# Layer norm of phase two: the bias moved from ScalarE to GpSimd, the two transposes given their own distance, and a new list of task times

## The chip, the cores and the metric

The kernel runs on one core of a Trainium2 chip. The core has five engines with a queue of instructions each, run strictly in order: TensorE (PE, matrix products; its weight loads are listed as PEld), VectorE (DVE), ScalarE (ACT), GpSimd (POOL) and SyncE (SP, which here only issues DMAs). An instruction starts when the one before it on its engine is out of the way and the semaphores it waits for have arrived. The metric is the device time of one execution in microseconds (us); a profile is one further execution, recorded instruction by instruction.

## The reference

A block of four layers on 4096 tokens (2 sequences of 2048) of 512 channels, all in float32, each with a layer norm in front and a residual around it:

```
x = x + attn_a(layernorm(x))     # RWKV recurrence over the tokens
x = x + ffn(layernorm(x))        # 1376 hidden, weights lut[idx]
x = x + attn_b(layernorm(x))     # Mamba: 1024 channels, 16 states, conv of 4
x = x + ffn(layernorm(x))        # the same weights
layernorm(x) = (x - mean) / sqrt(var + 1e-5)
```

The layer norm of one token is one multiplication and one addition per element: `x * rs + nm` with `rs = (var + eps) ** -0.5` and `nm = -mean * rs`. These two numbers per token are what the change is about.

## The kernel before

**Phases.** Phase one (the function's first `with` block) does the RWKV layer in 8 chunks of 512 tokens, and beside it looks up the weights of the ffn. Phase two does the other three layers in 16 chunks of 256 tokens (two tiles of 128 tokens, `NJ` = 2). The change lies in phase two alone.

**Order.** Phase two is written as a list of tasks with times. `line.at(t, fn, ...)` notes a task, and `Line.emit` calls them in order of time; each task issues its instructions to the engines' queues then and there. So the times fix nothing but the order on each engine; on the chip nobody looks at them. One stage `w` of the loop at the end of the phase is 32 units of time (`SLOTS`), and holds work of four chunks: the scan of chunk w, the output projection and second ffn of chunk w-1, the front of the Mamba layer (input projection, convolution, `x_product`) of chunk w+1, and the first ffn of chunk w+2. The dictionary `AT` holds the offsets of the tasks within the stage. Two tasks whose times come out equal are ordered by the order of `line.at` calls, or by the last bit of the sum `32 * w + offset` where rounding makes the two sums differ.

**The scan.** A stage has 32 items (2 halves of 4 channel tiles, by 4 groups of 4 states). Each item goes through: `grow` (POOL, L895 `db = du * B`, L898 adds the carried state), `decay` twice (ACT, L905, two exponentials into one of 3 PSUM buffers `dA`), `run` twice (DVE: the scan L915, the product with C L916, the copy of the last state L918), `fold` (POOL: L925, on half the items L930, L931, the sum over states). For each half, `step_size` makes the step sizes in two parts q = 0, 1: two products (PE L819), ACT L823 to L829 (with exponentials), `log` (ACT L833, a logarithm, tile `lt`), `correct` (DVE L836, L837, reads and writes `lt`), `close` (POOL L842 `dl`, L843 `du`), `carry` (ACT L850, an exponential, tile `h`), `cut` (POOL L857 `h`, L858). The tables of ScalarE for exponential, silu and logarithm differ, so a change between them issues an ACT_TABLE_LOAD.

**The layer norm** `ln(t, ci, box, to)` comes three times per stage: before the front (offset `frontln`; here "front norm"), before the second ffn (`f2ln`; "f2 norm"), before the first ffn (`f1ln`; "f1 norm"). `stats` (L639, L640 on DVE, L641 to L644 on POOL) gives mean and variance `mv`, then `rs` (add, L641; power, L642), then `nrs = -rs` (L644). `scale` issues for each tile j two ACT instructions: L650 makes `nm = mean * nrs` for 128 tokens, and L651 the normalized tile `xn`. `turn` transposes the tile on PE (4 products with the identity, L656, into PSUM tile `tr`) and copies it to SBUF on ACT (L657). The tiles j = 0, 1 are placed at `scale + 0.1 * j` and `turn + 0.1 * j`.

**Other names.** `x_product` (L795 on PE, then ACT copies L798 `bcs` and L800 `dtl`, then a DMA of `bcs` out and a broadcast back, L878) needs all of `u`, the silu of the convolution (ACT L781; the convolution's taps are DVE L775 on the product L755). `half`, `gate` and `close` of the ffn are L700 (PE, gate `pg` and up `gu`), L718 and L721 (ACT silu into `hT`), L727 and L730 (DVE); `residual` is L677 (PE, `po`) and L681 (DVE). The gate of the Mamba layer is L885 (PE) and L891 (ACT `sg`); `total` is L950 (ACT), the end of a scan half L961, L962 (DVE). Weights come through a ring of 18 buffers by DMAs of SP (L612).

Of the kernel before, what the change touches and what calls it, by code (L numbers as in the profile page):

```python
# [8 lines left out]
F32 = mybir.dt.float32  # L9
I32 = mybir.dt.int32  # L10
AF = mybir.ActivationFunctionType
ALU = mybir.AluOpType
# [3 lines left out]
P = 128  # L16
# [44 lines left out]
def block_kernel(ctx: ExitStack, tc: tile.TileContext, a: dict, out: bass.AP):  # L61
    nc = tc.nc
    V, S, G, PE = nc.vector, nc.scalar, nc.gpsimd, nc.tensor
# [33 lines left out]
    with ExitStack() as pa:  # L97
# [4 lines left out]
        small = pa.enter_context(tc.tile_pool(name="a_small", bufs=2))  # L102
# [23 lines left out]
        for k in range(4):  # L126
# [7 lines left out]
                  y=0.475, x=-3.69, stats=-2.901, stat=0.11, each=0.061, copy=0.089, fmul=0.561,  # L134
                  opened=-3.107, mean=-2.389, scale=-2.198, turn=-2.092, out=4.08, outs=0.018,
                  add=0.096, bits=(-4.21, 29.2), marks=(-4.03, 10.79), ahead=0.472, ff=(13.35,
                  31.01), place=-4.5, places=0.069, ffln=11.025, nextln=7.821, flast=1.489,
                  turned=2.527, fgate=0.173, fdown=2.314, times=0.273)
        NBITS = 8
        line = Line()  # L140
# [399 lines left out]
    with ExitStack() as pb:  # L540
# [13 lines left out]
        small = pb.enter_context(tc.tile_pool(name="b_small", bufs=2))  # L554
# [7 lines left out]
        def load_w():  # L562
# [4 lines left out]
        NJ = TB // P  # L567

        AT = dict(total=0.13, y=1.08, decay=1.1, grow=1.5, fold=2.75, gates=(2.59, 0.82, 24.96,
                  26.99), front=(6.05, 6.48, 7.41, 8.16), f2=(8.75, 8.93, 12.67, 14.17, 14.38,
                  16.88), f1=(21.88, 21.98, 24.35, 24.27, 29.8, 25.63), f2d=16.39, f1d=30.14,
                  x=11.42, step0=20.87, step1=9.48, step=2.56, exp=0.62, log=1.16, fix=2.12,
                  du=3.52, carry=3.52, zero=4.38, proj=2.49, frontln=3.04, f2ln=5.92, f1ln=18.95,
                  store=29.71, taps=1.03, conv=0.04, unit=1.86, add=0.6, silu=-0.29, hT=0.36,
                  scale=0.19, turn=0.82, g1ln=-5.01, g1=-0.28, g1s=1.51, late=8.22, step1a=-6.29,
                  ahead=12.53, spread=2.01, gsilu=0.64, bca=-1.73, step0a=22.65, fronta=(-0.27, 2.4,
                  1.42, 4.18), xa=14.67)
        line = Line()  # L580
        xs = {}

# [47 lines left out]
        def ln(t, ci, box, to=None):  # L630


            def stats():
                box["xnT"] = to if to is not None else tp.tile([P, KC, TB], F32, tag="xnT", name="xnT")
                st = small.tile([P, NJ, 6], F32, tag="st", name="st")
                mv = small.tile([P, NJ, 2], F32, tag="mv", name="mv")
                rs = small.tile([P, NJ, 1], F32, tag="rs", name="rs")
                for j in range(NJ):
                    V.bn_stats(st[:, j, :], xs[ci][j])  # L639
                    V.bn_aggr(mv[:, j, :], st[:, j, :])  # L640
                G.tensor_scalar(rs, mv[:, :, 1:2], EPS, None, ALU.add)  # L641
                G.tensor_tensor(rs[:, :, 0], rs[:, :, 0], mhalf[:, :NJ], ALU.pow)  # L642
                nrs = small.tile([P, NJ, 1], F32, tag="nrs", name="nrs")
                G.tensor_scalar(nrs, rs, -1.0, None, ALU.mult)  # L644
                box["mv"], box["rs"], box["nrs"] = mv, rs, nrs

            def scale(j):
                box["xn", j] = wk.tile([P, C], F32, tag="xn", name="xn")
                nm = small.tile([P, 1], F32, tag=f"nm{j}", name="nm")
                S.activation(nm, box["mv"][:, j, 0:1], AF.Copy, scale=box["nrs"][:, j, :])  # L650
                S.activation(box["xn", j], xs[ci][j], AF.Identity, bias=nm, scale=box["rs"][:, j, :])  # L651

            def turn(j):
                tr = mmp.tile([P, KC, P], F32, tag="mm", name="tr")
                for k in range(KC):
                    PE.transpose(tr[:, k, :], box["xn", j][:, k * P : (k + 1) * P], ident)  # L656
                S.copy(box["xnT"][:, :, j * P : (j + 1) * P], tr)  # L657

            line.at(t, stats)
            for j in range(NJ):  # L660
                line.at(t + AT["scale"] + 0.1 * j, scale, j)
                line.at(t + AT["turn"] + 0.1 * j, turn, j)

        def residual(times, ci, lhsT, src):

            po, n = [], len(times)
            w = [stream.piece(t, t + 0.01, src(i)) for i, t in enumerate(times)]

            def first():
                for j in range(NJ):  # L670
                    po.append(mmp.tile([P, C], F32, tag="mm", name="po"))

            def one(i):
                lw = lhsT(i)
                m = lw.shape[0]
                for j in range(NJ):
                    PE.matmul(po[j], lhsT=lw[:, j * P : (j + 1) * P], rhs=w[i]["w"][:m],  # L677
                              start=(i == 0), stop=(i == n - 1))

            def add(j):  # L680
                V.tensor_tensor(xs[ci][j], xs[ci][j], po[j], ALU.add)  # L681

            line.at(times[0], first)
            for i, t in enumerate(times):
                line.at(t + 0.005, one, i)
            for j in range(NJ):
                line.at(times[-1] + 0.3 + AT["add"] + 0.15 * j, add, j)

        def feed_forward(t_ln, times, td, dtd, ci, layer=1):

            box, hT, ps = {}, {}, {}
            if ci == 1 and layer == 0:
                box["xnT"] = ready[1]
            else:
                ln(t_ln, ci, box)
# [36 lines left out]
            for i, ti in zip(range(0, NF, 2), times):  # L732
                d = 0.65 if i + 1 < NF else 0.3
                for j in range(2):
# [3 lines left out]
                    line.at(tj + 0.005, half, i, j, w)  # L738
                line.at(ti + d + AT["silu"], gate, i)
                line.at(ti + 2 * d + AT["hT"], close, i)  # L740
            residual([td + dtd * i for i in range(NF)], ci, lambda i: hT[i], lambda i: wff[i][:, 2 * C :])

        def front(t_ln, times, tx, ci, box):

            box["xnT"] = ready[ci % 2]
            if ci:
                ln(t_ln, ci, box, ready[ci % 2])
# [35 lines left out]
            for cp, tp_ in enumerate(times):  # L783
                w = [stream.piece(tp_, tp_ + 0.01, a["in_proj"][2 * cp + j]) for j in range(2)]
                line.at(tp_ + 0.005, product, cp, w)
                line.at(tp_ + AT["conv"], copy, cp)
                for j in range(2):
# [205 lines left out]
        for w in range(-1, nchunk + 1):  # L993
            t = SLOTS * w
# [13 lines left out]
            if -1 <= w < nchunk - 1:  # L1008
                boxes[w + 1] = {}
                late = AT["late"] if w == 0 else 0.0  # L1010
# [70 lines left out]
```

## Time and profile before

| | |
|---|---|
| median of 3 executions | 3647.52 us (3642.11 to 3651.19) |
| profiled execution | 3645.21 us |
| its span, first to last instruction | 3643.4 us |
| TensorE clock granted, mean | 0.973 of full |
| phase one | about 0 to 700 us of the span |
| phase two | about 700 us to the end; 16 stages |
| length of a stage in the middle | 177.2 us (DMA of `bcs` issued at 1360.08, 1537.28, 1714.34 us) |

"Busy" of an engine is the time in which one of its instructions ran. A line of the timeline gives start, duration, engine, source line, operation, tiles, shapes, count; in square brackets stands the idle time of the engine before it and the instruction that ended it. "x16" counts records, and a float32 product on PE leaves two records. A line of the waits gives the waiting instruction, the one that released it, the total in us, how often, and the longest.

### The profile page before, as it was taken

To read this page: it belongs to the slowest core of one execution; us is meant where nothing else is said; L and a number is where in the kernel's file an instruction comes from. 1 tells how busy PE (TensorE), PEld (TensorE's weight loads), DVE (VectorE), ACT (ScalarE), POOL (GpSimd) and SP (SyncE) were. 2 spreads that over 40 slices of the span, in tenths; PEclk is the share of its full clock that TensorE was granted. 3 is DMA by queue.
4 is the path that set the end of the run, shared out by engine and by line. 5 is a ranking of instruction groups with operands and counts; after the bars stand their busy time and mean duration, and the time that the engine had idled before them with its cause. 6 is when DMAs were issued, how large, how long until landed. Compare 5 with 4: busy or idle time off the path is not lost. (4 is left out here: it accounts for less than half of the span.)

```text
span 3643.4 us, 43340 instructions
## 1 busy us (share of the span) xinstructions
PE 3398.7 (93%) x12592; PEld 2294.4 (63%) x12592; DVE 3231.3 (89%) x4880; ACT 2739.9 (75%) x4862; POOL 2979.1 (82%) x2803
## 2 busy tenths in 40 slices
PE   7998999887999999999999999999999999998698
PEld 3443444466676767677666766676767676766475
DVE  8999999568999999999999999998989898989882
ACT  5556766578787888888787878787878787878661
POOL 2445666378999999999999999999999999999850
PEclk9999999998999999999999999999999999999799
DMA  3111111254565656565656565656565655664442
GB/s 123 55 55 67 58 67 67 82 199 149 179 196 169 217 165 210 169 208 165 216 165 211 168 201 176 202 180 203 180 192 182 190 183 189 188 192 130 141 143 61
DMA packets 267148, 573.02 MB, mean 157 GB/s; under 512 B 29856, under 2 KB 31520, under 8 KB 266912
## 3 DMA queue, kind: packets, MB, share of 16 engines
q1 hardware_dynamic: 266112, 568.68, 49.0%
q8 instruction: 101, 1.65, 0.2%
q10 hardware_dynamic: 800, 1.57, 0.1%
q14 instruction: 135, 1.11, 0.1%
HBM read 543.66 MB, written 26.48 MB: 156 GB/s over the span
## 5 line engine op out<-in xcount | busy, mean ns | idle before, releaser
L915 DVE TENSOR_TENSOR_SCAN h<-h,db 128x512 f32<-128x512 f32 x1024 | 1252.5, 1223 | 124.6 <-ACT h L905 100.2
L895 POOL TENSOR_TENSOR db<-du,bc 128x1024 f32<-128x1024 f32 x512 | 1207.4, 2358 | 37.1 <-PE y L939 34.5
L905 ACT ACTIVATE h<-dl,acol 128x256 f32<-128x256 f32 x2048 | 956.2, 475 | 303.6 <-DVE hst L918 267.4
L916 DVE TENSOR_TENSOR db<-h,bc 128x512 f32<-128x512 f32 x1024 | 708.1, 691 | 35.9
L925 POOL TENSOR_TENSOR db<-db 128x512 f32<-128x512 f32 x480 | 609.9, 1271 | 0.0
L677 PE MATMUL po<-w,hT 128*128 128x512 f32 x1364 | 601.0, 592 | 0.0
L700 PE MATMUL pg<-xnT,w 128*128 128x256 f32 x2400 | 537.0, 381 | 1.1 <-ACT xnT L657 1.0
L700 PE MATMUL gu<-xnT,w 128*128 128x256 f32 x2400 | 537.6, 379 | 0.0
L700 PEld LDWEIGHTS pg<-xnT,w 128*128 128x128 f32 x2400 | 456.7, 191 | 67.5 <-ACT xnT L657 5.5
L700 PEld LDWEIGHTS gu<-xnT,w 128*128 128x128 f32 x2400 | 456.0, 190 | 68.0 <-issue 6.7
L677 PEld LDWEIGHTS po<-w,hT 128*128 128x128 f32 x1364 | 259.4, 190 | 287.9 <-issue 272.0
L931 POOL TENSOR_TENSOR acc<-db 128x256 f32<-128x256 f32 x480 | 349.3, 728 | 37.6
L403 PE MATMUL ps<-xnT,wrvk 128*128 128x512 f32 x768 | 343.5, 599 | 8.6 <-DVE e L428 8.5
L905 ACT ACT_TABLE_LOAD x206 | 264.3, 1283 | 3.7
L885 PE MATMUL ps<-ready,w 128*128 128x256 f32 x1024 | 235.6, 384 | 29.0 <-DVE x L681 14.5
L403 PEld LDWEIGHTS ps<-xnT,wrvk 128*128 128x128 f32 x768 | 146.7, 192 | 181.6 <-issue 162.8
L755 PE MATMUL ps<-ready,w 128*128 128x256 f32 x1024 | 238.2, 393 | 10.1 <-DMA w<-in_in_proj 8.4
L885 PEld LDWEIGHTS ps<-ready,w 128*128 128x128 f32 x1024 | 195.4, 192 | 73.9 <-DVE x L681 24.4
L677 PE MATMUL po<-w,u 128*128 128x512 f32 x512 | 236.8, 611 | 2.1 <-DVE u L962 2.1
L755 PEld LDWEIGHTS ps<-ready,w 128*128 128x128 f32 x1024 | 202.0, 199 | 45.8 <-issue 12.0
L775 DVE SCALAR_TENSOR_TENSOR ps<-xin,cw,ps 128x256 f32<-128x256 f32 x384 | 187.1, 487 | 29.9 <-ACT ps L769 19.5
L930 POOL TENSOR_TENSOR db<-db,acc 128x256 f32<-128x256 f32 x240 | 174.8, 729 | 18.8
(163 smaller groups left out, 4993.5 us busy)
## 6 DMA issues: line engine op xcount, KB each, us to landing
w<-wff SPq DMA_DIRECT2D x1023, 256.0 KB, 2.7
bc<-bcd SPq DMA_DIRECT2D x256, 512.0 KB, 4.4
w<-in_in_proj SPq DMA_DIRECT2D x256, 256.0 KB, 2.8
w<-in_out_proj SPq DMA_DIRECT2D x128, 256.0 KB, 2.8
w<-wff SPq DMA_DIRECT2D x11, 768.0 KB, 4.4
x<-in_x SPq DMA_DIRECT2D x8, 1024.0 KB, 5.4
x<-x1d SPq DMA_DIRECT2D x32, 256.0 KB, 3.5
out_x<-x SPq DMA_DIRECT2D x32, 256.0 KB, 6.7
```

The source lines that it names most:

```text
L403: PE.matmul(ps, lhsT=wrvk[:, k, lo : lo + P], rhs=chunk["xnT"][:, k, :], start=(k == 0), stop=(k == KC - 1))
L677: PE.matmul(po[j], lhsT=lw[:, j * P : (j + 1) * P], rhs=w[i]["w"][:m], start=(i == 0), stop=(i == n - 1))
L700: PE.matmul(to[:m], lhsT=w[:, k, :m], rhs=box["xnT"][:, k, :], start=(k == 0), stop=(k == KC - 1))
L755: PE.matmul(ps[cp][:, j, :], lhsT=wj[:, k, :], rhs=box["xnT"][:, k, :], start=(k == 0), stop=(k == KC - 1))
L775: V.scalar_tensor_tensor(ps[cp][:, j, :], xin[cp][:, j, i : i + TB], cw[:, c, i : i + 1], ps[cp][:, j, :], ALU.mult, ALU.add)
L885: PE.matmul(ps[:, j, :], lhsT=wj[:, k, :], rhs=box["xnT"][:, k, :], start=(k == 0), stop=(k == KC - 1))
L895: G.tensor_tensor(d, box["du", half][:, c4, :].unsqueeze(1).to_broadcast([P, 4, TB]), bs[half, q], ALU.mult)
L905: S.activation(h[:, n, :], box["dl", half][:, c4, :], AF.Exp, scale=acol[:, 4 * half + c4, col : col + 1])
L915: V.tensor_tensor_scan(flat(h), flat(h), flat(d[:, two, :]), 0.0, ALU.mult, ALU.add)
L916: V.tensor_tensor(d[:, two, :], h, cs[half, q][:, two, :], ALU.mult)
L925: G.tensor_tensor(d[:, 0:2, :], d[:, 0:2, :], d[:, 2:4, :], ALU.add)
L931: G.tensor_tensor(to, d[:, 0, :], d[:, 1, :], ALU.add)
```

## The change

`stats` now makes the bias itself, for both tiles at once, on GpSimd: a product of mean and `rs` and a multiplication by -1, in place of `nrs`. `scale` issues one ACT instruction per tile instead of two. The second tile's `turn` stands `turns` = 0.23 units after the first, where it was 0.1. And nearly all offsets of `AT` are new.

```
-        AT = dict(total=0.13, y=1.08, decay=1.1, grow=1.5, fold=2.75, gates=(2.59, 0.82, 24.96,
-                  26.99), front=(6.05, 6.48, 7.41, 8.16), f2=(8.75, 8.93, 12.67, 14.17, 14.38,
-                  16.88), f1=(21.88, 21.98, 24.35, 24.27, 29.8, 25.63), f2d=16.39, f1d=30.14,
-                  x=11.42, step0=20.87, step1=9.48, step=2.56, exp=0.62, log=1.16, fix=2.12,
-                  du=3.52, carry=3.52, zero=4.38, proj=2.49, frontln=3.04, f2ln=5.92, f1ln=18.95,
-                  store=29.71, taps=1.03, conv=0.04, unit=1.86, add=0.6, silu=-0.29, hT=0.36,
-                  scale=0.19, turn=0.82, g1ln=-5.01, g1=-0.28, g1s=1.51, late=8.22, step1a=-6.29,
-                  ahead=12.53, spread=2.01, gsilu=0.64, bca=-1.73, step0a=22.65, fronta=(-0.27, 2.4,
-                  1.42, 4.18), xa=14.67)
+        AT = dict(total=0.94, y=1.66, decay=1.09, grow=1.51, fold=2.58, gates=(2.5, -0.28, 25.02,
+                  27.07), front=(6.07, 6.51, 7.37, 8.21), f2=(8.68, 8.86, 12.67, 14.05, 14.38,
+                  16.88), f1=(21.55, 21.65, 24.43, 24.17, 30.07, 25.72), f2d=16.48, f1d=30.11,
+                  x=10.74, step0=20.72, step1=9.45, step=2.31, exp=0.42, log=1.48, fix=2.49, du=3.4,
+                  carry=3.48, zero=4.25, proj=2.39, frontln=3.23, f2ln=5.96, f1ln=18.6, store=31.98,
+                  taps=1.03, conv=0.18, unit=1.87, add=0.7, silu=-0.29, hT=0.4, scale=0.43,
+                  turn=1.03, g1ln=-0.46, g1=-0.26, g1s=1.39, late=8.05, step1a=-6.84, ahead=14.42,
+                  spread=2.95, gsilu=0.66, bca=1.47, step0a=22.97, fronta=(-0.56, 2.3, 0.72, 2.94),
+                  xa=15.45, turns=0.23)
...
                 G.tensor_scalar(rs, mv[:, :, 1:2], EPS, None, ALU.add)
                 G.tensor_tensor(rs[:, :, 0], rs[:, :, 0], mhalf[:, :NJ], ALU.pow)
-                nrs = small.tile([P, NJ, 1], F32, tag="nrs", name="nrs")
-                G.tensor_scalar(nrs, rs, -1.0, None, ALU.mult)
-                box["mv"], box["rs"], box["nrs"] = mv, rs, nrs
+                nm = small.tile([P, NJ, 1], F32, tag="nm", name="nm")
+                G.tensor_tensor(nm, mv[:, :, 0:1], rs, ALU.mult)
+                G.tensor_scalar(nm, nm, -1.0, None, ALU.mult)
+                box["rs"], box["nm"] = rs, nm
 
             def scale(j):
                 box["xn", j] = wk.tile([P, C], F32, tag="xn", name="xn")
-                nm = small.tile([P, 1], F32, tag=f"nm{j}", name="nm")
-                S.activation(nm, box["mv"][:, j, 0:1], AF.Copy, scale=box["nrs"][:, j, :])
-                S.activation(box["xn", j], xs[ci][j], AF.Identity, bias=nm, scale=box["rs"][:, j, :])
+                S.activation(box["xn", j], xs[ci][j], AF.Identity, bias=box["nm"][:, j, :], scale=box["rs"][:, j, :])
...
-                line.at(t + AT["turn"] + 0.1 * j, turn, j)
+                line.at(t + AT["turn"] + AT["turns"] * j, turn, j)
```

What the new offsets do to the order, as the two programs' instruction lists show it, in a stage of the middle:

- PE: the transposes of the front norm stand four records of `po` later, with four records between the two tiles. Those of the f1 norm have four records between them. Those of the f2 norm stay together. One gate product L885 moves eight `po` products earlier.
- ACT: the f2 norm's two `xn` have one `decay` between them. In the part of the stage that follows, the exponentials L827 and L829 of q = 0 stand ahead of the last `u` (they stood behind it), and the copies `bcs` and `dtl` and one `decay` stand ahead of the logarithm L833 of q = 0 (they stood behind it).
- ACT, stages 8 to 13 only: two silu L718 that followed each other directly now have a `decay` between them, at two places. The silu and the decay have equal times there (14.05 + 0.65 - 0.29 = 15.5 - 1.09 and 21.55 + 0.65 - 0.29 = 23 - 1.09), and rounding decides; in stages 1 to 7 it decides the other way. Stages 14 and 15 have this at the first place. In the whole program the table loads of ACT go from 601 to 629.
- POOL: in each half of the scan, `close` of q = 1 stands one `grow` earlier in the second half, and `close` and `cut` of q = 1 one whole item earlier in the first half of the next chunk. All else has its old order.
- DVE: one `run` changes places with an end of scan half (L961, L962) or with a single `hT`, `lt` at a few places; the norms' L639, L640 keep their place among the runs.
- SP: the store of a finished chunk stands twelve weight loads and no broadcast load later; two loads of gate weights stand four loads earlier.
- Beginning (stage -1, 0) and end (stage 15 and after): the order differs at single places, among them on PE at the end, where the products L939 (`spread`, the sum over states of the last chunk) stand later among the others.

## The prediction

> **What bounds the kernel now.** I read the engines' sums first. They point at PE:
>
> ```profile
> PE 3398.7 (93%) x12592; PEld 2294.4 (63%) x12592; DVE 3231.3 (89%) x4880; ACT 2739.9 (75%) x4862; POOL 2979.1 (82%) x2803
> ```
>
> This is an average over phases. The second view is the busy time in two middle stages, 1539 to 1893 us:
>
> ```profile
> core 0: us, PE busy (x) PEld busy (x) DVE busy (x) ACT busy (x) POOL busy (x), PEclk, DMA share, GB/s
> 1539.00:1893.00 354.00, 342.70 (x1350) 247.41 (x1349) 323.51 (x533) 288.70 (x528) 338.42 (x339) 1.00 0.61 188
> ```
>
> PE 342.7 and POOL 338.4 of 354: close. What tells them apart is who waits. The third view, the waits in stages 2 to 13 (1184 to 3311 us, 2127 us), POOL's and then PE's largest:
>
> ```profile
> POOL rs L641 <- DVE mv L640: 2.5, 7, 0.7
> POOL dl L842 <- DVE lt L837: 2.5, 1, 2.5
> POOL h L857 <- ACT h L850: 1.9, 5, 0.8
> POOL xin L762 <- DVE ps L775: 1.3, 1, 1.3
> ...
> ```
>
> ```profile
> PE tr L656 <- ACT xn L651: 39.2, 45, 1.6
> ...
> ```
>
> POOL waits 8.2 us in all, 0.7 a stage. Its other gaps are its own step from one instruction to the next: 0.08 us where the next one needs the last one's result. PE idles 62.7 us there, 5.2 a stage (39.2 on this line, 13.3 on L681). So POOL sets the stage length of 177.2 us, and PE's waits cost nothing.
>
> The fourth view, POOL's timeline, shows the norm and the two POOL instructions that could start to wait:
>
> ```profile
> 2556.69 0.22 POOL L641 TENSOR_SCALAR rs<-mv 128x2 f32<-128x2 f32 x1
> 2557.00 0.72 POOL L642 TENSOR_TENSOR rs<-rs,mhalf 128x2 f32<-128x2 f32 x1
> 2557.80 0.24 POOL L644 TENSOR_SCALAR nrs<-rs 128x2 f32<-128x2 f32 x1
> ...
> 2593.59 1.28 POOL L842 TENSOR_TENSOR dl<-dl,lt 128x512 f32<-128x512 f32 x1
> ...
> 2614.61 0.26 POOL L857 TENSOR_TENSOR h<-h,hst 128x32 f32<-128x32 f32 x1
> ```
>
> ACT starts the f2 norm's `nm` right at the end of `nrs`, and then runs without a wait for the next 32 us (its timeline):
>
> ```profile
> 2558.07 0.29 ACT L650 ACTIVATE nm<-mv,nrs 128x1 f32<-128x1 f32 x1 [1.95 <-POOL nrs L644]
> ...
> 2585.03 0.60 ACT L781 ACTIVATE u<-ps 128x512 f32<-128x512 f32 x1
> ...
> 2586.94 0.58 ACT L827 ACTIVATE ps<-ps 128x512 f32<-128x512 f32 x1
> ...
> 2588.05 0.98 ACT L905 ACTIVATE h<-dl,acol 128x256 f32<-128x256 f32 x2
> 2589.04 1.28 ACT L833 ACT_TABLE_LOAD   x1
> 2590.34 0.63 ACT L833 ACTIVATE lt<-w 128x512 f32<-128x512 f32 x1
> ...
> 2594.12 0.36 ACT L798 COPY bcs<-ps 32x256 f32<-32x256 f32 x1
> ...
> 2614.04 0.49 ACT L850 ACTIVATE h<-acol,dl 128x16 f32<-128x16 f32 x2
> ```
>
> DVE takes `lt` on (its timeline):
>
> ```profile
> 2592.82 0.69 DVE L837 TENSOR_TENSOR lt<-lt,ps 128x512 f32<-128x512 f32 x1
> ```
>
> It ends at 2593.51 and POOL's `dl` starts at 2593.59, the 0.08 of a direct follower: `close` is within a tenth of a microsecond of making POOL wait. Likewise L850 ends at 2614.53, and `cut` (L857) starts at 2614.61. So ACT's stretch from the f2 norm to `lt`, and on to `carry`, is a second chain without slack.
>
> **The change part by part.** All sums are against the profiled execution, 3645.2 us, which is 2.3 below the median of 3647.5; I don't correct for that.
>
> *1. POOL gets one instruction per norm*, the product mean times `rs`; the multiplication by -1 takes the place of `nrs`. Phase one has that product, on these engines:
>
> ```profile
> L262 POOL TENSOR_TENSOR nm<-rs,mv x11: 196/203/937, 31.9 to 693.1; 128x4 f32<-128x4 f32 x8, 128x2 f32<-128x2 f32 x3
> ```
>
> 0.203 + 0.083 to a dependent follower = 0.286 us. Of 45 norms, 42 lie where POOL is full (all but the first at 825 us and two at the end): **+12.0**. Low end: the 8.2 us of POOL waits absorb their part, +3.8. High end: each takes the 0.937 of the slowest record, 42 x 1.02 = 42.7. I take the median; three of those records have this very shape.
>
> *2. ACT's stretch from the f2 norm to `lt` of q = 0.* Removed: two L650, 0.33 + 0.31 with their steps, -0.64. Moved ahead of the last `u`: L827 and L829, 2586.94 to 2588.05 = +1.11. So `u` ends 28.03 us after the first `xn` starts. Now the wait that is added: `bcs`, `dtl` and one `decay` stand ahead of the logarithm, and `bcs` needs `x_product`, whose last 20 records need this `u`. PE's timeline:
>
> ```profile
> 2585.68 4.70 PE L795 MATMUL ps<-u,wxp 128*128 128x256 f32 x20 [0.50 <-ACT u L781]
> ```
>
> 28.03 + 0.05 + 4.70 = 32.8 us is the earliest `bcs`. ACT is there at 28.03 + 1.29 (table load) + 0.99 (`decay`) = 30.3: it waits 2.5 us, and behind it on ACT's queue are `lt` and all decays. Then 0.27 + 0.26 + 0.99 + 1.30 + 0.63: `lt` ends at 36.25, before at 32.90 (2558.07 to 2590.97). DVE's L837 and the steps add 0.80: `dl` can start 37.08 us after `xn` starts, which is 0.03 after `nm`. POOL, whose order between the two is unchanged, is there 35.55 us after its last norm instruction (2558.04 to 2593.59). It waits 1.53 us per stage. In stages 1 to 6 and 8 to 14 that is 13 x 1.53 = **+19.9** (in stage 7 the same distance has 1.67 of slack). Low end 0, if `u` comes earlier by that much; high end 3.35 x 14 = 47, the whole delay.
>
> *3. Two more table loads in stages 8 to 14*, between two silu and beside a decay: each 1.29 + 0.07 of step, 2.72 a stage, ahead of `carry` of q = 1. From `lt` to the end of L850 ACT took 23.56 (2590.97 to 2614.53). Minus `bcs` and `dtl` (0.52), minus two decays that now stand elsewhere (1.9): 21.1. So L850 would end 36.25 + 21.1 = 57.4 after `xn`, while POOL reaches `cut` at 56.57 - 0.13 + 1.53 = 57.97 with its own wait at `dl`: no wait in stages 1 to 7. With 2.72 more: 60.1, a wait of 2.2 us; 7 stages, **+15.4**. Low end 0 (the loads lie beside waits of ACT, which has 17 us a stage of its own idle time), high end 7 x 2.72 = 19. In exchange the waits of 0.1 to 0.3 at `cut` go: 13 x 0.2 = **-2.6**.
>
> Here the Trainium skill ("ScalarE: Activation LUTs", "What ACT_TABLE_LOAD costs") speaks against the change more than my row does: a switch is the load and a drain of about 1380 ns, 2.66 us together. In this trace the load at 2589.04 is followed by `lt` 1.30 later, with no drain to be seen. By the page the step would be some 18 us larger, as an estimate.
>
> *4. Costed at nothing.* At the front norm ACT waits 5.56 us for `nrs`, DVE then 3.48 for a decay and PE 1.57 and 0.38 for the tiles; two fewer ACT instructions and spread transposes shorten these (2.3 a stage on PE, with the f1 norm's second tile 0.38). POOL covers it: PE gets to the f2 norm earlier and waits there longer, 4 to 5 us, since that `xn` hangs on POOL. If POOL did not cover it, it would be worth -30 in 13 stages. First half of the scan: `dl` and `cut` have 5.4 to 9.5 us between ACT and POOL; `cut` of q = 1 moved one item earlier (4.65) and keeps some 3.7, with the two loads about 1.1. DVE's changed places: a run later by one 0.7 us instruction, under items that POOL folds some 15 us behind. SP's store behind twelve weight loads, and the gate loads earlier: issue of under 1 us, nothing reads the store. Beginning and end: 0, between -10 and +10, the larger part from L939, which waits 30.8 us for the last chunk before and still has to.
>
> **Sum:** 12.0 + 19.9 + 15.4 - 2.6 = +44.7: **3690 us**.
>
> **The rivals.** Changes under 0.3% (10.9 us) can't be told from none here.
>
> *A. PE sets the stage, and it gets faster (the other side).* Then PE's freed waits count, 2.3 x 13 = 30: 3615. For it: PE's 93%, its largest wait is exactly what the change shortens. Against it: POOL's 0.7 us of waits per stage. It decides from where POOL's idle time per stage exceeds the 0.86 us of its three new instructions and ACT's chain stays hidden; the trace has 0.7 and a `dl` without slack. Chance 0.09.
>
> *B. Only POOL's instruction counts.* ACT catches up, because it drops a wait elsewhere in the stretch, and `dl` doesn't wait: 3645.2 + 12.0 = 3657. For it: ACT is 82% busy. Against it: no wait of ACT lies between the f2 norm and `lt`. Chance 0.14.
>
> *C. The waits spread.* The first half's `cut` runs late in stages 8 to 13 too (up to 2.6 x 7 = 18), or the product on POOL takes 0.94 rather than 0.2 (+31): 3705 to 3740. For it: that cover is down to about 1 us. Chance 0.20.
>
> *D. Nothing measurable happens.* 3645, chance 0.04: terms 1 and 2 both swallowed.
>
> **How the numbers follow.** The forecast holds 0.53, with its own range 3675 to 3705 (one of its two waits half as large or half as large again). Faster by over 0.3%: A, 0.09. Within: D and half of B, 0.11. Slower: the forecast, C and the other half of B, 0.80. The range leaves out A, D, the lower third of B and the top of C: 3655 to 3722.
>
> **What the profile after would show.** POOL's L842 waiting for DVE's `lt` by about 1.5 us per stage, and from stage 8 its L857 for ACT's `h` by about 2.2; ACT waiting for PE at `bcs` (L798) by about 2.5; stages of 179.6 us early and some 181.8 from stage 8; 28 more table loads; `nm` on POOL at 0.20; PE's wait for `xn` gone from the front norm and larger at the f2 norm. I am wrong if the stage stays at 177 to 178, if `nm` takes 0.9, or if ACT has no wait at `bcs`. What would break it most easily is term 2: it is a difference of 1.5 us between two chains of 36.

## The result and the profile after

The changed kernel takes 3727.55 us (median; 3726.3 to 3728.07), the kernel before 3648.78: a ratio of 1.0226 (95% interval 1.0214 to 1.0238), or +79 us where +44.7 was forecast. It lies 5.6 us above the range. The profiled execution has a span of 3725.6 us, 82.2 more than before.

The sums of the engines hardly change; TensorE is busy 27 us longer with the same products:

```profile
PE 3426.0 (92%) x12577; PEld 2314.1 (62%) x12592; DVE 3235.4 (87%) x4880; ACT 2751.1 (74%) x4800; POOL 2987.6 (80%) x2848
```

The 12 stages that were read before (1184 to 3311 us there) now lie at 1199 to 3391. POOL's waits in them (waiting line, releaser, total us, times, longest) were 8.2 us in all and are 65.3:

```profile
POOL dl L842 <- DVE lt L837: 43.2, 13, 4.6
POOL h L857 <- ACT h L850: 14.5, 10, 2.7
POOL rs L642 <- DVE mv L641: 7.6, 6, 2.8
```

With 36 norms of one more POOL instruction (+10.1 us) that is 67 us more for 12 stages; their starts show +65. (The first line counts 13 waits, since the one of stage 2, 3.7 us, ends at the edge of the window; the 12 of stages 3 to 14 make 39.4.) The other 17 us lie ahead of stage 2 (its first `grow` starts 12.5 us later than before) and from stage 14 on.

ACT has two waits that were small or absent before (L765 had 6.5 us in 8 waits, L798 none):

```profile
...
ACT xin L765 <- PE ps L755: 33.4, 24, 2.3
ACT bcs L798 <- PE ps L795: 29.9, 12, 2.5
...
```

The second one is the wait that the prediction named. The first one it did not have. Stage 5 shows where it comes from. PE's timeline around the f2 norm, before:

```profile
1678.84 0.66 PE L656 MATMUL tr<-ident,xn 128*128 128x128 f32 x4 [1.55 <-ACT xn L651]
1679.87 0.66 PE L656 MATMUL tr<-ident,xn 128*128 128x128 f32 x4 [0.38 <-ACT xn L651]
1680.36 8.76 PE L755 MATMUL ps<-ready,w 128*128 128x256 f32 x32
```

and after:

```profile
1704.04 1.12 PE L656 MATMUL tr<-ident,xn 128*128 128x128 f32 x4 [4.15 <-ACT xn L651]
1705.66 1.12 PE L656 MATMUL tr<-ident,xn 128*128 128x128 f32 x4 [0.50 <-ACT xn L651]
1706.56 9.05 PE L755 MATMUL ps<-ready,w 128*128 128x256 f32 x32
```

PE waited 4.15 us for `xn`, where it had waited 1.55. After this wait four transposes take 1.12 us instead of 0.66, and 32 records of L755 take 9.05 us. With a full clock they take 7.07, in most stages of the kernel before; in this stage they took 8.76 there, so the clock was low before too, but only behind the transposes. The windows of the same stretch (busy times, then the granted clock, the DMA share and GB/s) say why:

```profile
core 0: us, PE busy (x) PEld busy (x) DVE busy (x) ACT busy (x) POOL busy (x), PEclk, DMA share, GB/s
...
1702.00:1716.00 14.00, 11.46 (x43) 9.61 (x44) 12.07 (x24) 10.67 (x23) 13.36 (x14) 0.76 0.26 75
...
```

The clock was 0.76 of full there: half from 1703.7 to 1710.6 us and full around that (before: half from 1680.8 to 1684.2). ACT's timeline of the same stage:

```profile
1703.18 0.81 ACT L651 ACTIVATE xn<-x,nm,rs 128x512 f32<-128x512 f32 x1 [4.88 <-POOL nm L646]
...
1712.19 0.59 ACT L765 COPY xin<-ps 128x512 f32<-128x512 f32 x1 [1.87 <-PE ps L755]
...
1732.54 0.60 ACT L781 ACTIVATE u<-ps 128x512 f32<-128x512 f32 x1
...
1737.93 0.36 ACT L798 COPY bcs<-ps 32x256 f32<-32x256 f32 x1 [2.49 <-PE ps L795]
...
1740.73 0.63 ACT L833 ACTIVATE lt<-w 128x512 f32<-128x512 f32 x1
...
```

DVE's and POOL's, at the end of the chain:

```profile
1741.40 0.69 DVE L837 TENSOR_TENSOR lt<-lt,ps 128x512 f32<-128x512 f32 x1 [3.30 <-ACT lt L833]
```

```profile
1742.16 1.27 POOL L842 TENSOR_TENSOR dl<-dl,lt 128x512 f32<-128x512 f32 x1 [3.46 <-DVE lt L837]
```

Read along the chain: L765 starts 1.87 us late, the last `u` ends 29.96 us after `xn` starts (28.03 forecast), `bcs` waits 2.49 (2.5), and `dl` makes POOL wait 3.46 (1.53). The excess at `dl` is the wait at L765. In stage 12 the clock over L755 was better (0.93), L765 waited 0.40, and `dl` 1.95. In both stages the difference is 1.55 to 1.6.

DVE's line bears on a reading of the prediction, that ACT's stretch from the f2 norm to `lt` had no slack before. Before, `lt` was written at 2590.97, and DVE took it at 2592.82, 1.85 us later, without a wait, straight behind its own work (1.57 to 1.86 in the stages 2 to 14). So what met POOL's `dl` within a tenth was DVE's queue, and ACT's stretch had some 1.6 to 1.9 us to spare. The forecast of 1.53 does not use that reading; after the change DVE does wait for `lt` (3.30 us), and ACT's stretch is the one that counts.

### The profile page after: what moved, and what is told of

It is laid out like the page before. It is cut to its first block, busy times and chain, and to the rows that moved or that the text cites. A ratio compares the mean times of both kernels' runs of the same rounds, so it can differ in the third digit from the quotient of the medians.

```text
span 3725.6 us, 43195 instructions
## 1 busy us (share of the span) xinstructions
PE 3426.0 (92%) x12577; PEld 2314.1 (62%) x12592; DVE 3235.4 (87%) x4880; ACT 2751.1 (74%) x4800; POOL 2987.6 (80%) x2848
## 3 DMA queue, kind: packets, MB, share of 16 engines
q10 hardware_dynamic: 800, 1.57, 0.1%
## 5 line engine op out<-in xcount | busy, mean ns | idle before, releaser
L755 PE MATMUL ps<-ready,w 128*128 128x256 f32 x1024 | 257.0, 415 | 9.1 <-DMA w<-in_in_proj 8.5
L755 PEld LDWEIGHTS ps<-ready,w 128*128 128x128 f32 x1024 | 216.5, 213 | 50.4 <-issue 12.0
L885 PE MATMUL ps<-ready,w 128*128 128x256 f32 x1024 | 233.5, 382 | 6.6 <-ACT sg L891 5.7
L885 PEld LDWEIGHTS ps<-ready,w 128*128 128x128 f32 x1024 | 195.9, 192 | 47.8 <-issue 13.4
```

Of the source, the lines that this page charges most:

```text
L755: PE.matmul(ps[cp][:, j, :], lhsT=wj[:, k, :], rhs=box["xnT"][:, k, :], start=(k == 0), stop=(k == KC - 1))
L885: PE.matmul(ps[:, j, :], lhsT=wj[:, k, :], rhs=box["xnT"][:, k, :], start=(k == 0), stop=(k == KC - 1))
```

## The experiments

The theory after the result has four costs: the logarithm behind `bcs` (1.5 us per stage), a slow TensorE clock after the f2 norm's wait (about 1.9), the split silu pairs (2.3 per stage from stage 8), and one more POOL instruction (0.28 per norm). The rivals: the clock is a companion, not a cause; the POOL instruction is what costs; PE or ACT bounds the kernel. Ratios are to the kernel before, run on the same chip.

**1. PE kept busy through the wait.**

```
             def turn(j):
...
+                for k in range(fill * (j == 0)):
+                    PE.matmul(tr, lhsT=ident, rhs=wdt[:, :C], start=True, stop=True)
                 for k in range(KC):
```

`fill` is 7 for the second ffn's norm and 0 for the others.

> The changed kernel, with 7 products of a constant weight added on PE ahead of the f2 norm's transposes in each stage; they write the tile that the transposes then overwrite, so no value changes, and they need nothing from ACT. They fill some 3.3 us of the 4.1 us that PE waits there for xn. Theory: in the changed kernel this wait makes the chip grant half the TensorE clock for a while after it, the transposes and the 32 products L755 come 2 us late, ACT waits for them at L765, and this is added to the wait of POOL's dl. Then here: L755 x32 back at 7.1 us (it took 7.6 to 9.6), the transposes at 0.66 (1.12), ACT's wait at L765 gone, POOL's wait at dl 1.55 instead of 3.4 per stage, time some 25 us shorter: about 3702. Rival: the clock is only a companion and the wait at dl comes from the order of ACT's instructions alone; then dl still waits 3.4 and the time is 3727 or longer by the added products.

Measured: 3708.83 us, ratio 1.0172 (1.0156 to 1.0187); the profiled execution took 3702.01. PE's timeline in stage 5:

```profile
1686.78 6.17 PE L654 MATMUL tr<-wdt,ident 128*128 128x512 f32 x14
1692.79 1.04 PE L656 MATMUL tr<-ident,xn 128*128 128x128 f32 x8
1693.66 7.07 PE L755 MATMUL ps<-ready,w 128*128 128x256 f32 x32
```

and POOL's waits over 1199 to 3391 us (the `dl` of stages 3 to 14; 39.4 in the changed kernel):

```profile
POOL dl L842 <- DVE lt L837: 22.2, 12, 4.2
POOL h L857 <- ACT h L850: 17.3, 15, 2.7
...
```

The seven products took 6.2 us, not the 3.3 that I had reckoned, and so filled the wait whole. The clock over L755 is 1.00 from stage 1 on, L755 takes 7.07 us, and `dl` waits 1.5 us in stages 2 to 6 and 10 to 14. The kernel has more work on PE, and it is faster: the clock is a cause, not a companion. The median is 19 us below the changed kernel's, the profiled execution 25, and some 25 were expected; in stages 1, 8 and 9, where the wait to be filled was shorter (1.9 to 3.3 us), the added products made PE late, L765 waits 0.76 to 1.81, and `dl` still waits over 3.

**2. The logarithm ahead of `bcs` again.**

```
-  x=10.74
+  x=11.42
```

> The changed kernel with x = 11.42 instead of 10.74: the copies bcs and dtl on ACT stand behind the logarithm of q = 0 again; nothing else changes on any engine. Theory (the wait of ACT for x_product ahead of the logarithm makes dl late): lt ends 4.0 us earlier, POOL's wait at dl goes from 3.4 to 0 in each stage, even with the slow clock; L857 in stages 8 to 14 waits about 3 instead of 2.3; time about 3688. Rival: the logarithm is late anyway (the product on POOL and the moved L827, L829 hold the chain), dl still waits over 1.5, time over 3710.

Measured: 3682.41 us, ratio 1.0097 (1.008 to 1.0114). POOL's waits in the same window:

```profile
POOL h L857 <- ACT h L850: 21.0, 18, 2.7
POOL rs L642 <- DVE mv L641: 10.3, 12, 1.6
POOL dl L842 <- DVE lt L837: 5.3, 6, 2.1
```

L765 still waits (33.1 us there), the clock over L755 is still 0.73 to 0.86 in all stages from 2 to 14 but one, and yet `dl` hardly waits. In the changed kernel its wait is L765's plus 1.55 us; here, where it waits at all (stage 8 apart), it is L765's minus 1.5 (0.94 and 2.42 in stage 2). So ACT's chain is 3 us shorter, where 4 were expected, and has 1.5 us of slack, which covers most of the slow clock. The two costs are not separate sums: the clock costs only because the chain has no slack, and the order of `bcs` and the logarithm took that slack. Stage 0 also loses its wait at L857 (4.3 us in the changed kernel): the better part of the changed kernel's late beginning was this same wait, since stage 0 starts 1.9 us late there and stage 1 9.4. (The start of stage 0, behind an unchanged phase one, lies between 757 and 769 us in all these profiles, so the 1.9 may be chance.)

**3. The silu pairs together.**

```
-  f2=(8.68, 8.86, 12.67, 14.05, ...), f1=(21.55, ...)
+  f2=(8.68, 8.86, 12.67, 14.06, ...), f1=(21.56, ...)
```

> The changed kernel with the last bits of two offsets moved (14.05 to 14.06, 21.55 to 21.56), so that in stages 8 to 14 the silu pairs stand together again, 31 table loads per stage; order changes on ACT alone. Theory: POOL's waits at L857 in stages 8 to 14 (2.3 each) go, and some of those at the front norm (7 us in all): 3727 - 15 to 20 = about 3709. Rival: the loads lay beside ACT's own waits, and what L857 waits for is the late logarithm: no change, 3725 to 3729.

Measured: 3701.5 us, ratio 1.0154 (1.0139 to 1.017), 26 us less, somewhat more than expected. POOL's waits:

```profile
POOL dl L842 <- DVE lt L837: 39.7, 12, 4.8
POOL h L857 <- ACT h L850: 1.2, 6, 0.4
POOL rs L642 <- DVE mv L641: 1.1, 1, 1.1
```

Both smaller lines of the changed kernel go: 13.3 and 6.5 us of the 26. Behind the window, L857's waits in stages 14 (2.2 us) and 15 (5.7 to 4.3) go or shrink too; `dl`, with the same 12 stages, is as before (39.7 and 39.4). The last line is not the front norm's, as the expectation has it, but the f1 norm's: it lies 115 to 125 us behind a stage's first `grow`, and DVE, which makes `mv`, waits there for the load of `x`. DVE's line of the changed kernel:

```profile
DVE st L640 <- DMA x<-x1d: 4.5, 6, 1.8
```

The prediction didn't have this wait. Here it goes with the split loads (but for stage 8), but they are not its only cause: runs 2 and 5 have it too, run 5 without any split load.

**4. The bias alone on GpSimd, task times of before.** In the kernel before, and with it one ACT instruction per tile:

```
-  G.tensor_scalar(nrs, rs, -1.0, None, ALU.mult)
+  G.tensor_tensor(nm, mv[:, :, 0:1], rs, ALU.mult)
+  G.tensor_scalar(nm, nm, -1.0, None, ALU.mult)
```

> The kernel before with only the bias formed on GpSimd (product and multiplication by -1 in place of nrs, one ACT instruction per tile), all task times as before. Theory: one more POOL instruction of 0.28 us in 42 norms, and ACT's chain 0.6 us shorter: +12, 3657 to 3661. Rival: this alone moves PE's wait to the f2 norm and brings the slow clock, so that dl waits too: over 3670. Other rival, ACT or PE sets the time: 3648 or less.

Measured: 3649.61 us, ratio 1.0011 (1.0002 to 1.0021): +4.8, where +12 was expected. The product takes its time on POOL:

```profile
L644 POOL TENSOR_TENSOR nm<-mv,rs x45: 194/194/196, 824.9 to 3578.1; 128x2 f32<-128x2 f32 x45
```

but from the start of stage 2 to that of stage 14 only 3.0 us are added, not 10. POOL's waits in the 12 stages fall by 3.4, from 8.2 to 4.8, of them 1.8 at `dl` and L857, which hang on ACT and DVE. The rest is no saving that the record can give to the edit: POOL's other instructions took 3.0 us less in this execution (0.15% of their sum, on another chip), and the steps between them 0.5. By the interval the edit costs between 0.7 and 7.7 us. PE waits once at the f2 norm, for 2.15 us (L754 here is L755 elsewhere):

```profile
1678.86 1.37 PE L655 MATMUL tr<-ident,xn 128*128 128x128 f32 x8 [2.14 <-ACT xn L650]
1680.06 8.76 PE L754 MATMUL ps<-ready,w 128*128 128x256 f32 x32
```

The clock over this line is 0.81 to 0.87 in 9 of the stages 2 to 14, with a wait of 0.05 to 0.27 at L765 and none at `dl`; stage 12 with 0.81 and stage 13 with a full clock both last 177.1 us. With the chain in its old order the slow clock costs nothing.

**5. The first three edits together.**

> The changed kernel with the three edits together: products on PE ahead of the f2 norm's transposes, bcs behind the logarithm, silu pairs unsplit. Theory: no wait at dl, none above 0.3 at L857; what stays of the change is the POOL instruction (+12 at most, +4 as measured alone) and about 1.2 us per stage of POOL's wait for the front norm's mv that showed when bcs alone was moved back: 3650 to 3665. Rival (one of the causes was only a companion of another, or something unnamed costs): 3675 or more.

Measured: 3661.78 us, ratio 1.0033 (1.002 to 1.0046). The waits of POOL from 1184 to 3311 us:

```profile
POOL rs L640 <- DVE mv L639: 8.6, 11, 2.3
POOL h L857 <- ACT h L850: 1.6, 2, 0.9
POOL dl L842 <- DVE lt L837: 1.1, 1, 1.1
```

The first line is the f1 norm's again. 15 us of the 79 are left (12 by the ratio); the three edits, which leave the norm and all other times as in the changed kernel, take away the rest. From the start of stage 2 to that of stage 14 it is 9.1 us more than before, and POOL's 36 added instructions take 10.1 there.

**6. The norm of before, with the new task times.** In the changed kernel, and with it two ACT instructions per tile:

```
-  G.tensor_tensor(nm, mv[:, :, 0:1], rs, ALU.mult)
-  G.tensor_scalar(nm, nm, -1.0, None, ALU.mult)
+  G.tensor_scalar(nrs, rs, -1.0, None, ALU.mult)
```

> The changed kernel with the norm of before (nrs on POOL, nm by two ACT instructions), all new task times kept. Theory: POOL gets 0.86 us per stage back, but ACT's chain from the f2 norm is 0.64 longer, and POOL waits for it at dl: the two nearly cancel, 3720 to 3732. Rival (the instruction on POOL costs its time wherever the waits are): 3727 - 12 = 3715 or less.

Measured: 3727.07 us, ratio 1.0216 (1.0199 to 1.0233): as the changed kernel. POOL's instruction is gone, and its wait at `dl` is larger:

```profile
POOL dl L843 <- DVE lt L838: 49.4, 12, 5.3
...
```

49.4 for 39.4 in the same stages 3 to 14: 0.83 us a stage, of which 0.18 is a longer wait at L765 and the rest the two instructions that ACT's chain got back. POOL's 0.86 a stage that became free went into that wait, so the two nearly cancel, as expected; the run cannot price them apart.

Runs 4 and 6 together separate the two halves of the change. The new norm with the old times is 0.1% slower than the kernel before, the old norm with the new times 2.2%, and both together 2.3%. So the loss comes from the list of task times, and hardly from the move of the bias.

**7 and 8. POOL given less work, from the kernel before.** Both add eps and negate the mean on DVE; 7 leaves the power alone on POOL and the bias on ACT, 8 has power and bias product on POOL:

```
-  G.tensor_scalar(rs, mv[:, :, 1:2], EPS, None, ALU.add)
+  V.tensor_scalar(rs, mv[:, :, 1:2], EPS, None, ALU.add)
+  V.tensor_scalar(nm, mv[:, :, 0:1], -1.0, None, ALU.mult)
   G.tensor_tensor(rs[:, :, 0], rs[:, :, 0], mhalf[:, :NJ], ALU.pow)
+  G.tensor_tensor(nm, nm, rs, ALU.mult)          # 8 only
```

> The kernel before with POOL's part of the norm cut to the power: eps added and the mean negated on DVE, nm on ACT as before (Copy of -mean scaled by rs). Theory (POOL sets the stage): 0.5 us less per norm on POOL, 1.5 per stage, 14 stages: -21, 3622 to 3630. Rival (PE sets it, or ACT's chain): within 4 us of before.

> The kernel before with eps added and the mean negated on DVE, power and bias product on POOL, one ACT instruction per tile. Theory: POOL loses 0.31 us per norm, 0.9 per stage, -13, and ACT's chain is 0.6 shorter, which takes away POOL's small waits too: 3627 to 3634. Rival (PE's wait for xn moves to the f2 norm, the clock drops, and the chain becomes late again): 3645 or more.

Measured: 7: 3634.37 us, ratio 0.9966 (0.9954 to 0.9978). 8: 3629.35 us, ratio 0.9948 (0.9933 to 0.9963), faster than both kernels. Taking work from POOL shortens the kernel, so POOL is the bound of before and PE's 93% is not. But 7 missed: it frees more of POOL and gains less. POOL's waits of 7, and then of 8 (2.5 at `dl` in the kernel before):

```profile
POOL dl L842 <- DVE lt L837: 17.6, 12, 3.3
...
```

```profile
POOL dl L841 <- DVE lt L836: 7.3, 12, 3.0
...
```

The second bound here is DVE's queue, not ACT's chain. In stage 5 of run 7 ACT wrote `lt` at 1714.43, and DVE took it 1.86 us later, without a wait, behind its own work:

```profile
1713.80 0.63 ACT L833 ACTIVATE lt<-w 128x512 f32<-128x512 f32 x1
```

```profile
1716.29 0.69 DVE L837 TENSOR_TENSOR lt<-lt,ps 128x512 f32<-128x512 f32 x1
```

```profile
1717.05 1.27 POOL L842 TENSOR_TENSOR dl<-dl,lt 128x512 f32<-128x512 f32 x1 [1.30 <-DVE lt L837]
```

DVE has two more instructions per norm, and from its last longer wait, for a decay behind the front norm, to L837 it needs 46.3 us in run 7 (45.5 before). That decay comes earlier in run 8, in which ACT has one instruction less per tile: L837 then starts 77.3 us behind the stage's first `grow` (77.9 in 7), POOL with its extra product arrives later, and `dl` waits 0.4 instead of 1.3.

**9. The front norm's transposes back in their place.**

```
-  line.at(t + AT["turn"] + AT["turns"] * j, turn, j)
+  line.at(t + (AT["turn"] + AT["turns"] * j if to is None else 0.7 + 0.02 * j), turn, j)
```

> The changed kernel with the front norm's two transposes together and four po products earlier, as before (PE's order as before there; on ACT one decay less between the two copies); f2 and f1 norms unchanged. Theory: PE's 4.1 us wait at the f2 norm is there because PE no longer waits at the front norm and has four products less between the two norms; now it falls to about 2.2, and the rest of the idle time goes to the front norm. At 2.2 us the clock drops in some stages only (with the bias alone on GpSimd, PE waited 2.15 and had the slow clock in 8 of 13 stages): ACT's wait at L765 0 to 1.2 instead of 1.9, dl 1.55 to 2.8, time 3702 to 3717. Rival: the wait at the f2 norm comes from the longer stage, not from the place of the front transposes: still over 3.5 us, time as the changed kernel's.

Measured: 3716.76 us, ratio 1.0203 (1.0184 to 1.0221). PE in stage 5 (first the front norm's transposes, then the f2 norm's):

```profile
1681.90 1.90 PE L656 MATMUL tr<-ident,xn 128*128 128x128 f32 x8 [3.08 <-ACT xn L651]
1683.59 6.23 PE L677 MATMUL po<-w,u 128*128 128x512 f32 x12
...
1697.45 0.66 PE L656 MATMUL tr<-ident,xn 128*128 128x128 f32 x4 [0.73 <-ACT xn L651]
1699.07 0.66 PE L656 MATMUL tr<-ident,xn 128*128 128x128 f32 x4 [0.96 <-ACT xn L651]
1699.56 7.07 PE L755 MATMUL ps<-ready,w 128*128 128x256 f32 x32
```

PE's idle time has only moved, from the f2 norm to the front norm. There 12 records of `po` take 6.23 us (5.32 in the kernel before), which comes out of the wait at the f2 norm. That wait at the f2 norm is at most 2.2 us, the clock over L755 is full in 8 of the stages 2 to 14, and in these `dl` waits 1.5 us (3.4 in stage 8, where it was 4.6); in the other five 1.8 to 3.9. So it was the later and spread transposes of the front norm that put the idle time where the slow clock hurts. In time the run is 11 us below the changed kernel, at the long end of what was expected, and the two intervals overlap; the waits are the better evidence.

**10. Three products instead of seven in the wait.** To the kernel of run 1:

```
-  ln(t_ln, ci, box, fill=7 * layer)
+  ln(t_ln, ci, box, fill=3 * layer)
```

> As the run with PE kept busy, but 3 products of a constant weight instead of 7 ahead of the f2 norm's transposes: 1.4 us of the 4.1 filled, 2.7 left. If the slow clock depends on how long PE is idle, it comes in fewer stages or for shorter than with 4.1: mean clock over L755 between 0.8 and 1.0, dl between 1.5 and 3.4, time between 3702 and 3720. If any wait of some 2 us is enough, dl stays at 3.4 and the time at 3727.

Measured: 3710.64 us (2 runs), ratio 1.0177 (1.0157 to 1.0198). The three products leave 1.58 us of wait, not 2.7 (each takes 0.88). A second wait of 0.95 us follows between the two tiles; stage 4:

```profile
1518.48 0.66 PE L656 MATMUL tr<-ident,xn 128*128 128x128 f32 x4 [1.58 <-ACT xn L649]
1520.09 0.66 PE L656 MATMUL tr<-ident,xn 128*128 128x128 f32 x4 [0.95 <-ACT xn L649]
1520.58 8.76 PE L755 MATMUL ps<-ready,w 128*128 128x256 f32 x32
```

With these same two waits the clock over L755 is 0.81 to 0.86 in stages 3, 4, 6, 7, 10, 12, 13 and full in 2, 5, 11, 14; `dl` waits 2.5 to 2.7 in the first and 1.5 in the second.

## Why the prediction was wrong

The direction and the two forecast waits were right. The time lies just outside the range, since one cost was set to nothing.

- **POOL bounds the kernel, with ACT's chain from the f2 norm beside it:** right for POOL (runs 7, 8). ACT's chain was not without slack before: DVE took `lt` 1.6 to 1.9 us after ACT had written it, and it is DVE's queue that met POOL. In the changed kernel ACT's chain is the second bound (runs 2, 6).
- **Step 1, one POOL instruction per norm, +12.0:** the size was right (0.197 us, in steps of 0.28), and POOL's own time grew by it. As a price of the norm's move it was too high: alone the move cost 4.8 (0.7 to 7.7), near the low end of 3.8, with POOL's waits 3.4 shorter. In the new order the move makes no difference that run 6 can tell, since what POOL loses ACT's chain gains.
- **Step 2, `bcs` ahead of the logarithm, +19.9:** right: ACT waited 2.49 (2.5 forecast), and `dl` 1.5 (1.53) as soon as the clock was full. Stage 7, which was left out for its 1.67 of slack, waited too: with the clock full 1.3 us (run 1).
- **Step 3, split silu, +15.4:** right in size at L857 (2.3 per stage, 2.2 forecast), and the small waits there did go. Run 3 gave 26 with the wait at the f1 norm, which was costed at nothing. The 17 us a stage of ACT's idle time, on which its low end leans, are some 33 by the prediction's own second view.
- **Step 4 is the one that failed:** "POOL covers it: PE gets to the f2 norm earlier and waits there longer, 4 to 5 us". PE did wait 4.15 us. But the sentence treated a wait of PE as free because PE was not the bound. After it, TensorE ran slowly for some microseconds, and the work in those was the front of ACT's chain. This added what L765 waits, 0.4 to 2.5 us per stage in stages 1 to 14, 24 us in all: `dl` waits 47.2 us there, before 3.2, and 19.9 of the 44 were forecast. The trace of before had the sign of it: in stages 3, 4, 5, 9 and 14 L755 took 8.4 to 8.8 us instead of 7.07, at a clock of 0.81 to 0.84, and L765 waited 0.25 for it. The prediction's timeline is of stage 10, in which the clock was full, and its mean over two stages, 1.00, hides 3.4 us of half clock.
- **The beginning, taken as 0:** measured +9 up to the first `grow` of stage 1, inside its bounds; run 2 showed that 4.3 of it was step 2 in stage 0.

Together: 44.7 forecast, 24 for the clock, 4 at the f1 norm (POOL's waits for `mv` in stages 1 to 14) and 9 at the beginning make 82, as much as the profiled span grew. That the measured time lies in the range of rival C (the waits spread) is luck: neither of its two reasons came true, since `nm` took 0.197 us and the first half's `cut` did not wait in stages 8 to 13. Rival A is refuted by runs 1, 7 and 8: adding products to PE made the kernel faster, and taking work from POOL did too.

The Trainium skill ("TensorE: Matmul & The Clock Gate", "What's actually happening") says that TensorE falls to half clock after an idle window of about 3.4 us, and that the windows run freely. The 4.15 us here and run 1, which fills it, agree. But under "Why this matters for your kernels" it asks only to avoid gaps above about 3 us, and in run 4 single waits of 2.15 us were followed by a clock of 0.81 to 0.87 in nine stages, in run 10 two waits of 1.58 and 0.95 us by 0.81 to 0.86 in seven. The measurement decides: shorter gaps can be enough, in some stages and not in others.

## What to carry to other kernels

An engine that is not the bound may wait for nothing, unless the wait changes how fast it runs afterwards: ask what TensorE does in the 10 us behind each longer wait, and who waits for that. Read the granted clock over the same stretch in several stages, not in one, since it differs from stage to stage with the same work. Where chains meet within a microsecond or two, a delay has no price of its own: the same slow clock cost 24 us in one order and next to nothing in the other. Before a chain is called tight, look when its last result was ready, not only when the next engine took it: `lt` lay there for 1.85 us. And where a change has two halves, run each alone: here the new norm made 0.1%, the new times 2.2%.

## What the runs showed of the hardware

- The clock after a wait of TensorE: with 2.5 to 4.2 us of waiting at the f2 norm, 0.74 to 0.93 over the 7.6 to 9.5 us of L755 in the stages 2 to 14 of the changed kernel; with one wait of 2.15 us (run 4), 0.81 to 0.87 in nine stages and full in three; with 1.58 and 0.95 us (run 10), 0.81 to 0.86 in seven and full in four; with 1.55 and 0.38 us (the kernel before), 0.81 to 0.84 in five and full in three; with the wait filled (run 1), full in all of these.
- Small instructions on DVE: the addition of eps to 128x2 values took 0.65 us (median, run 7), directly behind the statistics that it reads; the negation after it, of the same size, 0.155.
